# Cross attention's last block: score halves in turn, subtractions in a row, and block 13's last scaling and product behind the sums

## The chip, the cores and the metric

The kernel runs on one core of one Trainium2 chip. The metric is the device time of one execution in microseconds (us). A core has five engines that run side by side and wait for each other through semaphores: TensorE (PE in the profile, with its weight loads as PEld), VectorE (DVE), ScalarE (ACT), GpSimd (POOL) and SyncE (SP, which issues DMAs here).

## The reference, cut to what matters

One layer of a perceiver: cross attention of x to a long context, then self attention with relative positions, then a gated attention block. All in float32. The change is in the cross attention (and in the place of one step of the position table). What it computes:

```python
q = (layernorm(x) @ Wq + bq)        # x: 4 x 128 x 512, 16 heads of 32
k = (ctx @ Wk + bk)                 # ctx: 4 x 2048 x 512
v = (ctx @ Wv + bv)
scores = einsum('bqhd,bkhd->hbqk', q, k) / sqrt(32)
attn = softmax(scores.reshape(16 * 4, 128, 2048), axis=0)
x = x + einsum('hbqk,bkhd->bqhd', attn, v) @ Wo + bo
```

The softmax goes over heads and batch together (axis 0, 64 values for each pair of a query and a key), not over the keys. So each key's column is normalised by itself, and blocks of keys are independent until their products with v are added up.

## The kernel before, in words

The 2048 keys are cut into NK = 16 blocks of 128. In a block n the scores of all 16 heads and 4 batches are held as four tiles `sg[n, c]`, c = 0 to 3, of 128 keys by 2048 (4 heads x 4 batches x 128 queries). The order of the instructions on each engine is the order in which the program writes them (the section is under a manual schedule); the tile framework adds only the waits. The steps for one quarter (n, c), by function name and line:

- `keys` (L278) and `values` (L287): two projections of the context block on PE, four matmuls each, into one of two PSUM banks of a pool that they share (`bank`, L265); ACT copies the result out (L285, L291) and POOL adds the value's bias (L292). The v tiles have a pool of nine buffers.
- `scores` (L294): 16 small matmuls into two PSUM tiles of two banks each, called halves. `scores_out` (L314) is ACT's copy of one half to `sg`. `largest_of` (L317) is DVE's running maximum over one half, read from PSUM. In blocks 0 and 1 the program writes copy of half 1, maximum of half 0, copy of half 0, maximum of half 1. In later blocks it writes both copies first, and both maxima later, from `largest` (L326).
- `largest_tail` (L338) ends the maximum of a block on DVE (2 us). `shifted` (L345 through `over`) subtracts it from a quarter, `exponentials_of` (L354) is ACT's exponential of a quarter, `total` (L363) adds the quarter to the sum of its block on POOL, two folds of 128x1024 for a quarter (L360, L361), one for the first quarter (L358). `total_tail` (L371) ends the sum on POOL, `inverse` (L376) is DVE's reciprocal.
- `scaled` (L345 again) multiplies a quarter by the inverse on DVE; `attend` (L380) is the product with v, 16 matmuls of 32 columns, into a PSUM bank; `accumulate` (L396 on, L402 is its add) adds that bank to `acc` on DVE. Products without a bank of their own go to one bank with a single buffer, so each waits there for the accumulation of the one before.

The loop (L444) is a pipeline over blocks: in iteration n it makes the scores of block n, shifts and exponentiates block n-1, and scales and multiplies block n-2. A product is held back by one quarter (`done`): (n-2, c-1) is issued in quarter c. In the last iteration, n = 15, the values of block 15 begin (L450), since there are no keys left to make.

After the loop comes the tail (L493 on, m = 14, n = 15): the last product of block 13 (L494), block 15's maximum, shifts and exponentials with the remaining value projections between them, block 14's inverse and scalings. The sum of block 15 is divided: POOL adds quarters 0 and 1 and the first half of quarter 2 (`half_total`, L368), and PE adds the rest, and POOL's result, by products with the identity matrix into a PSUM bank (`sum_up`, L520). PE also puts x into the four output banks by identity products (L517). L538 folds the sum's bank to the normaliser z of block 15; then follow its inverse, the scalings of block 15, its products on top of block 14's in the same banks (`onto`), accumulations, and the output projection `project_out` (L542) in pieces between them. The next layer norm reads the output banks.

`position_table` (L110) is a generator whose three steps are placed in the first blocks: GpSimd's preparation (L438), a row product with its trip through DRAM (L469), and a product with a flip matrix, copied by ACT to `pos` (L141, L142), which the change moves. `pos` is first read in the self attention, at 708 us.

## Time and profile before

Three runs took 874.06, 872.05 and 871.6 us, median 872.05. The profiled execution took 871.75 us by itself; its span from the first to the last instruction is 869.8 us, at a mean granted clock of 0.986.

| engine | busy us | share of the span | instructions |
|---|---|---|---|
| PE | 831.1 | 96% | 7109 |
| DVE | 625.6 | 72% | 617 |
| ACT | 438.8 | 50% | 730 |
| POOL | 437.9 | 50% | 295 |

| part of the kernel, from the timelines | us from the span's start |
|---|---|
| first scores of block 0 | 44.6 |
| last scores (block 15, quarter 3) | 600.5 |
| normaliser of block 15 (L538) | 628.3 |
| first accumulation of block 15 | 633.6 |
| first statistics of the next layer norm | 653.2 |
| first projection of the self attention | 661.5 |

In the profile a row of the timeline is one instruction or a run of equal ones, with the idle time of its engine before it and the releaser in brackets. A busy share says little here, since it is the mean over stages; the order of the instructions is fixed on each engine, so the question at each point is which of several engines arrives last. The granted clock is PE's: at 0.50 the same matmul takes about twice as long.

### The profile page before, as it was taken

What the parts mean: (1) busy time and instruction counts of PE and PEld (TensorE: products, weight loads), DVE (VectorE), ACT (ScalarE), POOL (GpSimd) and SP (SyncE); (2) the same over time, 40 slices, a digit from 0 to 9 for tenths busy, and PEclk for the clock granted to TensorE, in tenths of its full rate; (3) what the DMA queues carried; (4) which work ended last, traced back from release to release, by engine and by line L of the source; (5) the groups of instructions that cost most, each with busy time, mean ns of one, the idle gap of its engine ahead of it and who ended that gap; (6) DMA issues with size and microseconds to landing.
All of it is one profiled execution on the core that took longest, in us unless ns stands there. A gap on an engine that the chain in (4) does not pass through costs nothing. (4 is left out here: it accounts for less than half of the span.)

```text
span 869.8 us, 16501 instructions
## 1 busy us (share of the span) xinstructions
PE 831.1 (96%) x7109; PEld 450.1 (52%) x7109; DVE 625.6 (72%) x617; ACT 438.8 (50%) x730; POOL 437.9 (50%) x295
## 2 busy tenths in 40 slices
PE   9999999999999999999999999999989996779998
PEld 5454544554544545545554544544445565566564
DVE  2049688888888888988878888888963537556563
ACT  3358446465465455455464464554403555844671
POOL 1246766666757567666566757567700022512152
PEclk9999999999999999999999999999999999789999
DMA  8140010110101001010110101001101203002101
GB/s 301 34 142 2 1 49 2 49 50 1 50 1 49 11 39 50 1 50 1 50 49 2 49 2 49 2 1 50 48 2 49 96 4 146 2 2 50 50 2 49
DMA packets 10906, 35.55 MB, mean 41 GB/s; under 512 B 977, under 2 KB 1138, under 8 KB 8786
## 3 DMA queue, kind: packets, MB, share of 16 engines
q1 hardware_dynamic: 8402, 29.43, 9.5%
q10 hardware_dynamic: 1632, 3.15, 1.0%
q0 software_dynamic: 800, 1.93, 0.9%
q8 instruction: 56, 0.92, 0.4%
q14 instruction: 16, 0.13, 0.0%
HBM read 33.45 MB, written 1.05 MB: 40 GB/s over the span
## 5 line engine op out<-in xcount | busy, mean ns | idle before, releaser
L345 DVE TENSOR_TENSOR sg<-sg,stat 128x2048 f32<-128x2048 f32 x128 | 288.2, 2281 | 1.2
L354 ACT ACTIVATE sg<-sg 128x2048 f32<-128x2048 f32 x64 | 122.4, 1912 | 244.9 <-DVE sg L345 244.9
L244 PE MATMUL ps_v<-w_xattn_Wv,ct 128*128 128x512 f32 x512 | 232.6, 598 | 3.6 <-ACT v L291 3.3
L237 PE MATMUL ps_k<-ct,w_xattn_Wk 128*128 128x512 f32 x480 | 221.9, 605 | 0.8 <-ACT pos L142 0.8
L360 POOL TENSOR_TENSOR sm<-sm,sg 128x1024 f32<-128x1024 f32 x46 | 108.6, 2360 | 145.5 <-ACT sg L354 143.3
L324 DVE TENSOR_TENSOR mx<-mx,ps_s 128x1024 f32<-128x1024 f32 x96 | 117.2, 1221 | 78.1 <-ACT sg L315 65.9
L244 PEld LDWEIGHTS ps_v<-w_xattn_Wv,ct 128*128 128x128 f32 x512 | 96.3, 191 | 130.6 <-issue 113.9
L237 PEld LDWEIGHTS ps_k<-ct,w_xattn_Wk 128*128 128x128 f32 x480 | 86.2, 189 | 94.1 <-issue 86.1
L315 ACT COPY sg<-ps_s 128x1024 f32<-128x1024 f32 x128 | 124.2, 1020 | 7.2 <-DVE mx L322 3.5
L361 POOL TENSOR_TENSOR sm<-sm,sg 128x1024 f32<-128x1024 f32 x46 | 108.8, 2366 | 3.6
L292 POOL TENSOR_TENSOR v<-v,row_xattn_bv 128x512 f32<-128x512 f32 x64 | 81.7, 1277 | 41.4 <-ACT v L291 38.0
L302 PE MATMUL ps_s<-qT,kT 32*128 32x128 f32 x2048 | 75.7, 283 | 0.1
L389 PEld LDWEIGHTS pso<-sg,v 128*32 128x32 f32 x1920 | 49.2, 110 | 47.5 <-DVE mx L324 22.0
L302 PEld LDWEIGHTS ps_s<-qT,kT 32*128 32x128 f32 x2048 | 63.3, 186 | 18.0 <-issue 17.0
L389 PE MATMUL pso<-sg,v 128*32 128x128 f32 x1920 | 65.3, 277 | 3.7 <-DVE acc L402 2.1
L358 POOL TENSOR_TENSOR sm<-sg 128x1024 f32<-128x1024 f32 x16 | 37.9, 2366 | 45.3 <-ACT sg L354 45.2
L656 POOL TENSOR_TENSOR lg<-lg,pos 128x512 f32<-128x512 f32 x6 | 7.4, 1263 | 85.9 <-ACT lg L655 85.9
L285 ACT ACTIVATE kT<-ps_k,bk 128x512 f32<-128x512 f32 x64 | 44.2, 694 | 11.9 <-PE ps_k L237 6.0
L291 ACT COPY v<-ps_v 128x512 f32<-128x512 f32 x64 | 36.4, 569 | 10.1 <-PE ps_v L244 10.1
L402 DVE TENSOR_TENSOR acc<-pso,acc 128x512 f32<-128x512 f32 x54 | 36.9, 682 | 3.9 <-PE pso L389 3.9
L322 DVE TENSOR_TENSOR mx<-sg,ps_s 128x1024 f32<-128x1024 f32 x16 | 19.5, 1220 | 27.3 <-ACT sg L315 27.3
L995 POOL TENSOR_TENSOR e<-e,rs 128x512 f32<-128x512 f32 x16 | 16.3, 1041 | 40.6 <-DVE rs L994 40.6
(213 smaller groups left out, 834.7 us busy)
## 6 DMA issues: line engine op xcount, KB each, us to landing
ct<-in_ctxT SPq DMA_DIRECT2D x15, 1024.0 KB, 4.9
ev_win<-in_tabv SPq DMA_DIRECT2D x1, 2048.0 KB, 9.3
w_xattn_Wk<-in_xattn_Wk ACTq DMA_DIRECT2D x4, 256.0 KB, 7.9
ct<-in_ctxT SPq DMA_DIRECT2D x4, 256.0 KB, 6.5
x<-in_x SPq DMA_DIRECT2D x4, 256.0 KB, 8.0
w_xattn_Wv<-in_xattn_Wv ACTq DMA_DIRECT2D x1, 1024.0 KB
w_xattn_Wq<-in_xattn_Wq SPq DMA_DIRECT2D x1, 1024.0 KB, 10.4
w_xattn_Wo<-in_xattn_Wo ACTq DMA_DIRECT2D x1, 1024.0 KB, 5.3
```

The lines of the kernel that those rows point to most:

```text
L237: nc.tensor.matmul(ps, lhsT=w[:, k, c * P : (c + 1) * P], rhs=src[:, k, :], start=(k == 0), stop=(k == C - 1))
L244: nc.tensor.matmul(ps, lhsT=src[:, k, b * T : (b + 1) * T], rhs=w[:, k, :], start=(k == 0), stop=(k == C - 1))
L285: nc.scalar.activation(kT[n, c], ps, AF.Identity, bias=bk[:, c : c + 1])
L292: nc.gpsimd.tensor_tensor(v[n, b], v[n, b], bv_row, ALU.add)
L302: nc.tensor.matmul(ps[i][:, cols], lhsT=kT[n, c][rows, cols], rhs=qT[rows, c, cols], start=True, stop=True)
L315: nc.scalar.copy(sg[n, c][:, k * HALF : (k + 1) * HALF], pss[n, c][k])
L324: nc.vector.tensor_tensor(mxs[n], mxs[n], pss[n, c][k], ALU.max)
L345: nc.vector.tensor_tensor(g, g, stat[:, row, :].unsqueeze(1).to_broadcast([P, NH * B, T]), op)
L354: nc.scalar.activation(sg[n, c], sg[n, c], AF.Exp, scale=SCALE)
L360: eng.tensor_tensor(t, t, g[:, 0:HALF], ALU.add)
L361: eng.tensor_tensor(t, t, g[:, HALF:], ALU.add)
L389: nc.tensor.matmul(ps[i * HD : (i + 1) * HD, b * T : (b + 1) * T], lhsT=v[n, b][:, h * HD : (h + 1) * HD], rhs=sg[n, c][:, f * T : (f + 1) ...
```

## The change

Nothing is computed differently in kind. The order in the last iteration and in the tail changes, and the sum of block 15 is divided otherwise between POOL and PE:

- Values 1 to 3 of block 15 go to the four temporary buffers that the layer norms use for `xn`, not to the pool of v tiles.
- The last scores, (15, 3), are copied and searched half by half in turn, as in blocks 0 and 1.
- In that quarter, exponential and sum of (14, 3) come behind the scores. A `break` leaves out the rest of it: scaling (13, 3) and accumulation (13, 2) move to the tail.
- The tail makes values 1 and 2 at once, then four subtractions in a row with their exponentials (values 3 behind the first), and only then scaling (13, 3), accumulation (13, 2), inverse of block 14 and scaling (14, 0).
- `half_total` is gone: POOL adds quarters 0 and 1, PE quarters 2 and 3 whole.
- The product (13, 3) comes behind the sums, its accumulation behind scaling (15, 0). Product (14, 0) has a bank of the shared pool, (14, 1) too; (14, 2) is in the single bank and comes behind product (15, 0).
- The third step of the position table comes at the end of block 0, not in block 1.

The diff:

```diff
         def values(n, b):
-            v[n, b] = vp.tile([P, D], F32, tag="v", name=f"v{n}_{b}")
+            if n == NK - 1 and b:
+                v[n, b] = tmp.tile([P, D], F32, tag="xn", name=f"v{n}_{b}")
+            else:
+                v[n, b] = vp.tile([P, D], F32, tag="v", name=f"v{n}_{b}")
...
             sg[n, c] = sc.tile([P, NH * B * T], F32, tag="sg", name=f"sg{n}_{c}")
-            if n < 2:
+            if n < 2 or (n, c) == (NK - 1, C - 1):
                 for k in (1, 0):
                     scores_out(n, c, k)
                     largest_of(n, c, 1 - k)
...
         def largest(n, c):
-            if n >= 2:
+            if n >= 2 and (n, c) != (NK - 1, C - 1):
                 largest_of(n, c, 0)
                 largest_of(n, c, 1)
...
-        def half_total(n, c):
-            nc.gpsimd.tensor_tensor(sms[n], sms[n], sg[n, c][:, 0:HALF], ALU.add)
...
                     shifted(n - 1, c)
-                    if n > 1:
+                    if n > 1 and (n, c) != (NK - 1, C - 1):
                         exponentials_of(n - 1, c)
                         total(n - 1, c)
...
                 if n == 0 and c == 0:
                     next(position)
+                if n == 0 and c == C - 1:
+                    next(position)
...
                     exponentials_of(0, c)
                     total(0, c)
-                    if c == 0:
-                        next(position)
+                if (n, c) == (NK - 1, C - 1):
+                    exponentials_of(n - 1, c)
+                    total(n - 1, c)
                 if n and c == C - 1:
                     total_tail(nc.gpsimd, n - 1)
                 if n >= 2:
                     if c == 0:
                         inverse(n - 2)
+                    if (n, c) == (NK - 1, C - 1):
+                        break
                     scaled(n - 2, c)
...
-        m, n = NK - 2, NK - 1
-        attend(*done)
+        l, m, n = NK - 3, NK - 2, NK - 1
         largest_tail(n)
         values(n, 1)
-        shifted(n, 0)
-        exponentials_of(n, 0)
-        total(n, 0)
+        values(n, 2)
+        for c in range(C):
+            shifted(n, c)
+            exponentials_of(n, c)
+            if c == 0:
+                values(n, 3)
+            if c < 2:
+                total(n, c)
+        scaled(l, C - 1)
         accumulate(*done)
-        values(n, 2)
-        shifted(n, 1)
-        exponentials_of(n, 1)
-        total(n, 1)
-        shifted(n, 2)
-        exponentials_of(n, 2)
-        values(n, 3)
-        half_total(n, 2)
-        shifted(n, 3)
-        exponentials_of(n, 3)
         inverse(m)
         scaled(m, 0)
-        scaled(m, 1)
...
-        sum_up(sg[n, 2][:, HALF:], True, False)
+        sum_up(sg[n, 2], True, False)
         sum_up(sg[n, 3], False, False)
         sum_up(sms[n], False, True)
-        attend(m, 0)
-        attend(m, 1, bank("m1"))
+        attend(l, C - 1)
+        attend(m, 0, bank("m0"))
+        scaled(m, 1)
         scaled(m, 2)
...
         inverse(n)
-        attend(m, 2, bank("m2"))
+        attend(m, 1, bank("m1"))
...
         scaled(n, 0)
+        accumulate(l, C - 1)
         attend(n, 0, pso[m, 0], True)
         accumulate(n, 0)
         scaled(n, 1)
+        attend(m, 2)
         project_out(0, range(B - 1))
         attend(n, 1, pso[m, 1], True)
```

## The prediction

> **What bounds the kernel now.** I read the busy shares first: PE 96%, DVE 72%, ACT and POOL 50%. The chain of waits is of no help ahead of 626 us; it starts there. So I read each engine's timeline over the change's stage, 590 to 656 us, and then the same span cut at the edges of the clock. DVE, from the last scores to the normaliser (columns: start, duration, line, operation, then in brackets the idle time before it and what ended it):

> ```profile
> 605.25 2.54 DVE L324 TENSOR_TENSOR mx<-mx,ps_s 128x1024 f32<-128x1024 f32 x2 [1.54 <-ACT sg L315]
> 607.83 1.95 DVE L339 TENSOR_REDUCE stat<-mx 128x128 f32<-128x1024 f32 x1
> 609.82 2.29 DVE L345 TENSOR_TENSOR sg<-sg,stat 128x2048 f32<-128x2048 f32 x1
> 612.02 0.68 DVE L402 TENSOR_TENSOR acc<-pso,acc 128x512 f32<-128x512 f32 x1
> 612.62 6.67 DVE L345 TENSOR_TENSOR sg<-sg,stat 128x2048 f32<-128x2048 f32 x3
> 619.40 0.96 DVE L376 RECIPROCAL stat<-z 128x128 f32<-128x128 f32 x1
> 620.40 6.68 DVE L345 TENSOR_TENSOR sg<-sg,stat 128x2048 f32<-128x2048 f32 x3
> 628.27 0.69 DVE L538 TENSOR_REDUCE z<-ps_sum 128x128 f32<-128x512 f32 x1 [1.19 <-PE ps_sum L523]
> ```

> DVE idles 1.54 us for ACT's copies of the last scores, then works without a break to 627.08. PE over the same time:

> ```profile
> 603.76 1.69 PE L389 MATMUL pso<-sg,v 128*32 128x128 f32 x32 [2.07 <-DVE acc L402]
> 605.38 11.60 PE L244 MATMUL ps_v<-w_xattn_Wv,ct 128*128 128x512 f32 x24
> ...
> 620.25 5.31 PE L523 MATMUL ps_sum<-sg,ident 128*128 128x512 f32 x12
> 626.25 1.98 PE L523 MATMUL ps_sum<-sm,ident 128*128 128x512 f32 x4 [0.69 <-POOL sm L369]
> ...
> 632.40 1.08 PE L389 MATMUL pso<-sg,v 128*32 128x128 f32 x32 [1.42 <-DVE sg L345]
> 634.30 4.54 PE L544 MATMUL ps_out<-w_xattn_Wo,acc 128*128 128x512 f32 x6 [0.81 <-DVE acc L402]
> ```

> The normaliser (628.27) waits for PE's last four sums, and these for POOL's half_total (L369). POOL's run depends on the exponentials, and they on the subtractions. The six projections at 634.30 take 0.76 us each; the same line's later ones follow each other every 0.43. The windows say why (columns: stretch, length, PE busy, PEld, DVE, ACT, POOL, granted clock, DMA share, GB/s):

> ```profile
> 600.69:604.10 3.41, 1.34 (x44) 1.15 (x48) 3.02 (x3) 3.09 (x3) 1.60 (x2) 1.00 0.00 0
> 604.10:607.51 3.41, 3.41 (x31) 1.99 (x24) 2.15 (x2) 1.12 (x2) 3.33 (x2) 0.50 0.02 5
> 631.41:634.82 3.41, 1.60 (x33) 1.11 (x34) 2.21 (x3) 0.00 (x0) 0.00 (x0) 1.00 0.00 0
> 634.82:638.23 3.41, 3.41 (x5) 1.35 (x4) 1.62 (x1) 0.00 (x0) 0.00 (x0) 0.50 0.00 0
> 720.15:723.57 3.42, 1.82 (x19) 1.61 (x16) 2.48 (x4) 0.00 (x0) 0.00 (x0) 1.00 1.05 385
> ```

> A stretch with PE busy 1.34 or 1.60 us of 3.41 (39%, 47%) is followed by one at half clock; one with 1.82 (53%) is not. Both half-clock stretches last 3.41 us and begin nine such lengths apart.

> **Part by part, ahead of the normaliser.** Times are on this profile's scale.

> *Last scores by halves.* They end at 600.52+1.17 = 601.69. For the alternation the row is the first block, which already has it:

> ```profile
> 51.04 2.54 DVE L324 TENSOR_TENSOR mx<-mx,ps_s 128x1024 f32<-128x1024 f32 x2 [2.96 <-PE ps_s L302]
> ```

> There the scores start at 49.83, DVE follows their end by 0.04 us, and the second ACT copy, at 52.29, waits for the first maximum. In that block's last scores the reduction follows their start by 63.09-59.30 = 3.79 us. So the reduction begins at 604.31 (was 607.83) and, 1.99 us later, the first subtraction at 606.30 (was 609.82): 3.5 us earlier. ACT's copies end at 603.99, and the exponential of block 14's last quarter, now behind them, at 605.8 (was 602.92).

> *Four subtractions in a row.* 2.29+3x2.20 = 8.9: 615.2. Then what was moved behind: scaling (13,3) 2.2, accumulation 0.7, inverse with its gap 1.0, three scalings 6.7: 625.8. DVE is ready for the normaliser then.

> *PE* no longer waits 2.07 us at 603.76: the product (13,3) is moved behind the sums, so the three value projections start at 601.7. Without the wait their stretch isn't under half busy, and 24x0.43 = 10.3: 612.0 (was 617.0). The identity products of x take 3.4: 615.4.

> *ACT.* Its in-order queue puts the copy of values 3 ahead of exponential 1. It ends at 612.7; three exponentials at 1.82 spacing end at 614.5, 616.35 and 618.2. The sums start at 616.4 and are 16 instead of 12, 16x0.43 = 6.9: 623.3.

> *POOL* loses half_total (2.36) but starts the fold of (14,3) at 605.85 instead of 603.06. Two folds 4.75, tail 2.58, three bias adds 3x1.24, one fold 2.35, two folds 4.75: 624.0. This is the last to arrive. PE's last four sums take 2.0: 626.05, and the normaliser starts at **626.07** (was 628.27): 2.2 us. The margins are thin: PE alone would allow 625.1, DVE 625.8.

> **Behind the normaliser.** Inverse and scaling follow as before, so product (15,0) starts at 630.20. PE waits 1.4 us for it as now. Its accumulation ends at 632.05; in its shadow PE does the moved product (14,2), 1.05, to 632.25, in place of the 0.81 wait. So the stretch has 1.4 us idle at most, at least 2.0 of 3.41 busy (59%), over the 1.82 that kept the clock. Six projections 6x0.43 = 2.57: 634.85; product (15,1) 1.05: 635.9; accumulation 0.7: 636.6; two scalings 4.45: 641.05; accumulation 0.65: 641.7. Before, this one ended at 645.61. **3.9 us**, of which 1.7 come behind the normaliser; from here on the order is the same.

> [...] The window rows show the drop after 1.60 us busy; I take the rows. [...] the grid may fall elsewhere in another run, and then before has no drop there to lose.

> *The position table's third step* moves from block 1 to the end of block 0. Its ACT copy (0.26 us, 71.23) delays the next by 0.15, and POOL's folds follow that exponential without a break to 93.15, where DVE waits for them: 0.15 us gained, bounds 0 and 0.26. The 0.81 us PE waits for that copy is worth nothing: at 131.71 PE waits 1.58 for ACT anyway. The moved product waits for nothing: POOL had seen posr landed by 55.34, and it is needed after 60.4.

> *At nothing:* values 1 to 3 in temporary buffers, last read by transposes before 27 us, next written after product (15,3) is done. Product (14,0) takes values 3's bank (copied 612.7), (14,1) the sum's (read 626.8, needed 627), (14,2) the single product bank (free 630.75, needed 631.2); (14,3) waits there for the accumulation ending 641.7, but PE comes to it at 644.3. Late banks would each cost the difference. SP's load of the next Wk, at 617.01, only waits for the last value projection and goes earlier; nothing is behind it.

> **Sum.** 3.9+0.15 = 4.05. The profiled execution took 871.75 (span 869.8 and 1.95 around it): 867.7. The median of the runs, 872.05, is 0.3 above it; I predict 868.0.

> **Rivals.**
> *A, as worked out:* 868.0, chance 0.62.
> *B, the clock part fails:* the grid spares the typical run before, or still catches the one after. For it: a margin of 0.2 us between 1.60 and 1.82, and a spread of 2.5 us over three runs. Against: the profiled run has the drop and is within 0.3 of the median. Gain 2.35: 869.7. Chance 0.24.
> *C, POOL keeps the old end:* its folds end at 626.2 again; only 1.7+0.15 remain: 870.2. For it: POOL is the last of three. Against: its durations hardly vary (2350 to 2390 ns). Chance 0.06.
> *D, more:* A with half-clock stretches of the later stages (740 to 747, 754 to 757, 778 to 785) falling shorter, 1.5 us: 866.5. Chance 0.05.
> *E, slower:* PE's clock is halved during the value projections. Then ACT's copy of values 3 holds up the exponentials: wholly at half clock projections end at 622.3, exponentials at 628.5, sums at 635.3, the normaliser 7.1 us later than before; less 1.85 this is 5.3 slower: 877.3. It decides from 4.9 us of delay at the projections (PE has 0.95 to spare, the whole gain is 3.9). Against: no wait is left ahead of them. Chance 0.03.

> **Range.** Within 0.3% is 2.6 us, about what a measurement can tell from no change: 869.4 to 874.7. A lies below in nine of ten (0.57), B in four of ten (0.10), D wholly: faster 0.73. Same: the rest of A and B and C, 0.24. Slower: E, 0.03. The low end takes D, the high end B and C: 866.3 to 870.6.

> **What would show it.** The first subtraction 3.5 us earlier, four in a row; no PE idle time ahead of the value projections; the last sums waiting for POOL, the normaliser 2.2 us earlier; the first six projections every 0.43 us; the moved product between (15,0) and them. Wrong if PE waits again for ACT or a bank, or the stretch after the sums is under half busy.

## The result, and the profile after

| kernel | median of 20 runs, us | lowest to highest | profiled execution (span) |
|---|---|---|---|
| before | 872.0 | 869.43 to 874.06 | 871.75 (869.8) |
| after | 868.5 | 867.86 to 872.27 | 870.22 (868.3) |

The ratio of the times is 0.9974, with a 95% interval of 0.9963 to 0.9985: 2.3 us less, between 1.3 and 3.2. This is the distance of the means of the 20 runs (871.5 and 869.2). The medians lie 3.5 us apart. That these two numbers differ, and that the two profiled executions are only 1.5 us apart, is the main question below.

DVE's timeline after, in the same stretch as the one shown of before (line numbers have moved: L328 is the maximum, L349 subtraction and scaling, L539 the normaliser):

```profile
600.99 2.55 DVE L328 TENSOR_TENSOR mx<-mx,ps_s 128x1024 f32<-128x1024 f32 x2 [0.81 <-PE ps_s L306]
603.57 1.97 DVE L343 TENSOR_REDUCE stat<-mx 128x128 f32<-128x1024 f32 x1
605.58 11.08 DVE L349 TENSOR_TENSOR sg<-sg,stat 128x2048 f32<-128x2048 f32 x5
616.57 0.68 DVE L403 TENSOR_TENSOR acc<-pso,acc 128x512 f32<-128x512 f32 x1
617.17 0.95 DVE L377 RECIPROCAL stat<-z 128x128 f32<-128x128 f32 x1
618.16 6.68 DVE L349 TENSOR_TENSOR sg<-sg,stat 128x2048 f32<-128x2048 f32 x3
625.72 0.69 DVE L539 TENSOR_REDUCE z<-ps_sum 128x128 f32<-128x512 f32 x1 [0.88 <-PE ps_sum L523]
```

The maximum now waits for the scores, not for ACT. The run of five is the four subtractions and scaling (13,3). The last scores start at 599.78 here and at 600.52 before, so times are compared from there: the first subtraction comes 5.80 us behind them (9.30 before), the normaliser 25.94 (27.75). PE, after:

```profile
600.88 10.57 PE L244 MATMUL ps_v<-w_xattn_Wv,ct 128*128 128x512 f32 x24
611.29 3.60 PE L517 MATMUL ps_out<-x,ident 128*128 128x512 f32 x8
615.74 7.13 PE L523 MATMUL ps_sum<-sg,ident 128*128 128x512 f32 x16 [0.85 <-ACT sg L358]
623.70 1.98 PE L523 MATMUL ps_sum<-sm,ident 128*128 128x512 f32 x4 [0.83 <-POOL sm L365]
...
629.88 1.08 PE L390 MATMUL ps_m<-sg,v 128*32 128x128 f32 x32 [1.45 <-DVE sg L349]
630.78 1.06 PE L390 MATMUL pso<-sg,v 128*32 128x128 f32 x32
631.78 2.84 PE L545 MATMUL ps_out<-w_xattn_Wo,acc 128*128 128x512 f32 x6
```

No wait is left ahead of the value projections. The last four sums wait for POOL, as forecast. The moved product (630.78) fills PE's time up to the projections, and six of these take 2.84 us instead of 4.54.

But for the position table's step the rest of the kernel wasn't touched. The whole of each profiled execution, in stretches:

| from, to (us) | before | after |
|---|---|---|
| start to last scores of block 0 | 59.30 | 58.66 |
| last scores of block 0 to last scores of block 15 | 541.22 | 541.12 |
| last scores of block 15 to normaliser | 27.75 | 25.94 |
| normaliser to first statistics of the next layer norm | 24.95 | 23.28 |
| these statistics to the first projection of self attention | 8.28 | 8.37 |
| first projection of self attention to the end | 208.3 | 210.9 |

The tail gained 1.81 and 1.67 us; self attention, with the same instructions, lost 2.6. The 0.64 us at the start is not the change's: nothing was moved there, and over the eleven profiles of this case this stretch takes 58.42 to 59.53 us. Two neighbouring stretches of the clock in self attention, after (columns as in the prediction's window rows):

```profile
715.39:718.80 3.41, 1.81 (x33) 1.49 (x30) 2.49 (x4) 0.00 (x0) 0.06 (x1) 1.00 0.89 300
718.80:722.22 3.42, 3.42 (x40) 3.09 (x40) 0.00 (x0) 0.00 (x0) 0.00 (x0) 0.50 1.07 452
```

The second is a half-clock stretch that the profile of before doesn't have. PE was busy for 1.81 us ahead of it; the row of before with 1.82 us was followed by full clock. So at 1.81 and 1.82 us (53%) PE's busy time does not tell whether the clock falls.

### The profile page after: what moved, and what is told of

It reads as the page before. It is cut to its first block, busy times and chain, and to the rows that moved or that the text cites. A ratio compares the mean times of both kernels' runs of the same rounds, so it can differ in the third digit from the quotient of the medians.

```text
span 868.3 us, 16503 instructions
## 1 busy us (share of the span) xinstructions
PE 831.1 (96%) x7113; PEld 451.0 (52%) x7113; DVE 625.5 (72%) x617; ACT 438.8 (51%) x730; POOL 435.8 (50%) x294
## 3 DMA queue, kind: packets, MB, share of 16 engines
HBM read 33.45 MB, written 1.05 MB: 40 GB/s over the span
## 4 chain that ended last, share of the span: by engine, by line
DVE 34%; PE 34%; ACT 20%; issue 10%; POOL 2%; DVEq 0%; ACTq 0%; POOLq 0%
DVE sg L349 14%; DVE mx L328 11%; ACT sg L319 10%; PE ps_v L244 4%; ACT sg L358 3%; PE s_k L237 3%; DVE stat L343 3%; ACT v L295 3%; PE ps_k L237 3%; DVE mx L326 2%; PE s_v L671 2%; PE s_y L1085 2%; PE s_q L237 2%; PE ps_q L237 2%; PE s_q L244 2%
## 5 line engine op out<-in xcount | busy, mean ns | idle before, releaser
L349 DVE TENSOR_TENSOR sg<-sg,stat 128x2048 f32<-128x2048 f32 x128 | 288.1, 2282 | 1.2
L244 PE MATMUL ps_v<-w_xattn_Wv,ct 128*128 128x512 f32 x512 | 231.5, 596 | 3.7 <-ACT v L295 3.7
L328 DVE TENSOR_TENSOR mx<-mx,ps_s 128x1024 f32<-128x1024 f32 x96 | 117.2, 1221 | 77.2 <-ACT sg L319 64.2
L244 PEld LDWEIGHTS ps_v<-w_xattn_Wv,ct 128*128 128x128 f32 x512 | 95.8, 190 | 129.9 <-issue 112.8
```

The costliest lines, as they stand in the source:

```text
L244: nc.tensor.matmul(ps, lhsT=src[:, k, b * T : (b + 1) * T], rhs=w[:, k, :], start=(k == 0), stop=(k == C - 1))
L328: nc.vector.tensor_tensor(mxs[n], mxs[n], pss[n, c][k], ALU.max)
L349: nc.vector.tensor_tensor(g, g, stat[:, row, :].unsqueeze(1).to_broadcast([P, NH * B, T]), op)
```

## The experiments

**Does the clock differ between runs of one kernel?** The kernel before, unchanged.

> The kernel before, unchanged, for a second trace and for each run's granted clock. Theory (grid): the windows of the clock lie anew in each run, so times fall in groups some 2 us apart (869.5, 872, 874 so far), the groups with the lower mean clock are the slower ones, and a run of the 869.5 group has a mean clock near 0.99 instead of 0.986. Rival (fixed): the clock is the same in each run, and the spread has another cause, so clock and time do not go together.

The ratio to the kernel before is 1.0003, from 0.9991 to 1.0015. Clock and time go together in its 22 runs:

| mean granted clock | runs | us |
|---|---|---|
| 0.990 | 4 | 869.02 to 869.52 |
| 0.986 or 0.987 | 12 | 870.87 to 872.57 |
| 0.983 or 0.984 | 6 | 872.10 to 874.55 |

Its profiled execution was one of 869.17. PE behind the sums in it:

```profile
631.57 1.08 PE L389 MATMUL pso<-sg,v 128*32 128x128 f32 x32 [1.42 <-DVE sg L345]
633.46 2.84 PE L544 MATMUL ps_out<-w_xattn_Wo,acc 128*128 128x512 f32 x6 [0.81 <-DVE acc L402]
```

Both waits stand there, 1.42 and 0.81 us as in the first profile, and yet the projections run at full clock: 2.84 us. From the normaliser to the next layer norm's first statistics it takes 23.25 us, as much as the changed kernel (23.28). There is no half-clock stretch at 604 either, and the normaliser comes 27.73 us behind the last scores, so the one there in the first profile cost nothing. The grid theory holds: reduced by whole stretches of 3.41 us, the edges of the clock lie 0.8 us from the span's start here and 3.3 us in the first profile. The rival falls. Four profiles have this tail without fillers (the two of before and two experiments below), and only the first has the drop in it.

**Is it PE's waiting that costs the clock?** Fill the two waits.

```diff
+        def keep_busy(k):
+            for _ in range(k):
+                nc.tensor.matmul(out_ps[0][:, 0:P], lhsT=warm, rhs=warm, start=False, stop=False)
...
+        keep_busy(5)
         attend(n, 0, pso[m, 0], True)
+        keep_busy(3)
         accumulate(n, 0)
```

> The kernel before with only PE kept busy in the two waits behind the normaliser: 5 and 3 matmuls that add zeros to an output bank (1.1 and 0.65 us) in the waits of 1.42 and 0.81 us. Theory (grid): no half-clock stretch at the first six projections, which follow each other every 0.43 us; from the normaliser to the accumulation of product (15,2) some 1.7 us less than in the profile of before (17.3 from start to start instead of 16.65 is ruled out: 14.9 to 15.0 in place of 16.65), and the group of runs at 872 shrinks, with a median near 870.0. Rival (the 1.7 us come from the new order of the products, not from the clock): 16.65 us as before, median 872.

```profile
630.44 1.38 PE L544 MATMUL ps_out<-warm 128*128 128x128 f32 x10
631.93 1.08 PE L389 MATMUL pso<-sg,v 128*32 128x128 f32 x32
632.94 0.94 PE L544 MATMUL ps_out<-warm 128*128 128x128 f32 x6
633.82 2.84 PE L548 MATMUL ps_out<-w_xattn_Wo,acc 128*128 128x512 f32 x6
```

`warm` holds zeros, so nothing is added. The waits are filled, nothing comes later, and from the normaliser to the accumulation of (15,2) it is 14.96 us, to the statistics 23.25. The ratio is 0.9986 (0.9974 to 0.9998), some 1.2 us less, with a median of 870.67, not 870.0. So the tail's part of the clock can be had with no reordering at all, and on the mean of runs it is worth somewhere between 0.2 and 2.3 us. An estimate narrows it. These are two positions of a stretch over the two waits in the second profile of before, the outermost with as little PE work as the 1.58 us ahead of the drop in the first (1.60 in the prediction's row, whose edges are 0.02 us off):

```profile
629.65:633.06 3.41, 1.58 (x52) 1.04 (x43) 2.21 (x2) 0.00 (x0) 0.00 (x0) 1.00 0.02 5
630.55:633.96 3.41, 1.58 (x33) 1.11 (x34) 2.21 (x3) 0.00 (x0) 0.00 (x0) 1.00 0.00 0
```

They lie 0.90 us apart, a quarter of 3.41. With 1.83 us as the limit, which kept the clock at 128.30 us in the profile of after, it is 1.40 us, four tenths; 1.88 us kept the clock at this place in the experiment with the position table's step alone. If all positions are equally likely, before has the drop in a quarter to four tenths of its executions, and it costs 0.4 to 0.7 us on average, not 1.7.

**Where did self attention lose its 2.6 us?** The changed kernel with PE kept busy there, and, for comparison, the kernel before with both sets of fillers. The edit of the later stage:

```diff
+        fill = bank_z("fill")[:, 0:P]
+        idle(fill, 6)
         ps = logits(0)
...
             if c + 1 < C:
+                if c < 2:
+                    idle(fill, 6)
                 ps = logits(c + 1)
...
                 if c:
+                    idle(fill, {(1, 3): 22, (2, 3): 3, (3, 0): 5}.get((c, i), 0))
                     transposed(c - 1, i)
...
+        idle_ps = bank_z("idle")[:, 0:P]
+        idle(idle_ps, 21)
         out_ps = [bank_q(f"out{b}") for b in range(B)]
...
-        idle_ps = bank_z("idle")[:, 0:P]
```

> The changed kernel with PE kept busy in the waits of the self attention's logits, exponentials and output (6 matmuls of zeros ahead of the first three sets of logits, 22, 3 and 5 ahead of three transposes, 21 ahead of the output's transposes), into a bank that nothing reads. Theory (grid): the half-clock stretches between 715 and 785 us go, at most one is left; self attention becomes shorter by 2 to 5 us, the mean clock over 0.995, and the runs' spread falls from 4.4 us to about 1; median 864 to 866. Rival (the later stages lost 2.7 us in the profiled execution through the change itself, its earlier weight loads for instance): they stay as long as in the profile of after, median 868 to 870.

> The kernel before with both sets of filling matmuls, those of the tail and those of the later stages. Theory (grid): a narrow spread like that of the changed kernel with the later filling, and slower than it by the order part of the change alone, 1.9 us (1.6 to 2.3). Rival (fixed): slower than it by 3.5 to 4.1 us.

| kernel | median us (6 runs each) | lowest to highest | self attention to the end, profile |
|---|---|---|---|
| before, both fillings | 867.81 | 867.30 to 868.18 | 206.28 |
| after, later filling | 865.59 | 865.24 to 866.59 | 206.71 |

The spread falls from about 5 us to 0.9 and 1.4, self attention is equal but for 0.4 us in both, and one half-clock stretch is left there in the changed kernel's profile, none in the other's. With the clock held so far, the change gains **2.2 us** (2.1 between the means), inside the forecast of 1.6 to 2.3 for its order part; the rival (3.5 to 4.1) falls. The later loss was the clock's, not the change's. The changed kernel's own runs say the same: 12 of the 20 had a mean clock of 0.990 (the profiled one 0.986) and took 867.86 to 868.51 us.

**Which edits carry the order part?** Four kernels with one thing changed each. First, the halves undone: both copies first, then both maxima.

```diff
-            if n < 2 or (n, c) == (NK - 1, C - 1):
+            if n < 2:
                 for k in (1, 0):
                     scores_out(n, c, k)
                     largest_of(n, c, 1 - k)
+            elif (n, c) == (NK - 1, C - 1):
+                for k in (1, 0):
+                    scores_out(n, c, k)
+                largest_of(n, c, 0)
+                largest_of(n, c, 1)
```

> The changed kernel with one part undone: the last scores are copied whole by ACT first, and both maxima follow. Theory (POOL's folds arrive last): the first subtraction comes 1.1 to 1.3 us later against the start of the last scores, but the exponential of (14,3) and POOL's run start up to 0.2 us earlier, so the normaliser is only 0.2 to 0.6 us later (26.1 to 26.5 us behind the start of the last scores instead of 25.94), then with DVE's scalings as the last arrival. Rival (the subtractions set the end): the normaliser is later by the same 1.1 to 1.3 us.

```profile
603.40 2.55 DVE L333 TENSOR_TENSOR mx<-mx,ps_s 128x1024 f32<-128x1024 f32 x2 [2.88 <-ACT sg L324]
605.98 1.96 DVE L348 TENSOR_REDUCE stat<-mx 128x128 f32<-128x1024 f32 x1
607.97 11.08 DVE L354 TENSOR_TENSOR sg<-sg,stat 128x2048 f32<-128x2048 f32 x5
...
620.55 6.68 DVE L354 TENSOR_TENSOR sg<-sg,stat 128x2048 f32<-128x2048 f32 x3
627.15 0.68 DVE L544 TENSOR_REDUCE z<-ps_sum 128x128 f32<-128x512 f32 x1
```

The last scores start at 600.12, so the first subtraction is 7.85 us behind them, 2.05 later than with the halves and not 1.1 to 1.3: the first maximum waits for both copies, since the half that it reads is copied last. The normaliser is 1.09 later (27.03). It now follows the scalings without a wait: DVE is the last to arrive, and of the 2.05 us DVE's former wait of 0.88 for PE took up most (0.96 with the 0.08 by which the two rows now overlap). Neither forecast holds: the theory's 0.2 to 0.6 us was too small, and the rival's 1.1 is met only as a number, since the subtraction moved by 2.05. That DVE would be the last was right: the halves are worth 1.1 us. The product behind the normaliser waits 2.33 us in this kernel, and the clock is half from 631.0 to 634.4.

Second, only the removal of half_total, in the kernel before.

```diff
-        half_total(n, 2)
...
-        sum_up(sg[n, 2][:, HALF:], True, False)
+        sum_up(sg[n, 2], True, False)
```

> The kernel before with one part of the change alone: no half_total on POOL, PE adds quarter 2 whole. Theory (the parts hold each other up): POOL is done 2.4 us earlier, but PE has four sum instructions more, and its value projections and identity products still end some 5 us later than in the changed kernel, so the normaliser stays within 0.4 us of before (27.75 us behind the start of the last scores). Rival (POOL's half_total alone held it up): 1.5 to 2.2 us earlier.

```profile
603.14 1.08 PE L389 MATMUL pso<-sg,v 128*32 128x128 f32 x32 [2.07 <-DVE acc L402]
604.15 10.57 PE L244 MATMUL ps_v<-w_xattn_Wv,ct 128*128 128x512 f32 x24
614.55 3.60 PE L516 MATMUL ps_out<-x,ident 128*128 128x512 f32 x8
618.53 7.13 PE L522 MATMUL ps_sum<-sg,ident 128*128 128x512 f32 x16 [0.38 <-ACT sg L354]
625.50 1.88 PE L522 MATMUL ps_sum<-sm,ident 128*128 128x512 f32 x4
```

The last four sums wait for nothing now, but PE itself is late. The normaliser comes 27.52 us behind the last scores, 0.23 earlier (0.21 against the second profile of before, which has full clock in the projections as this one has), and the rival's 1.5 to 2.2 falls. Third, the opposite: half_total put back into the changed kernel.

```diff
             if c < 2:
                 total(n, c)
+            if c == 2:
+                nc.gpsimd.tensor_tensor(sms[n], sms[n], sg[n, c][:, 0:HALF], ALU.add)
...
-        sum_up(sg[n, 2], True, False)
+        sum_up(sg[n, 2][:, HALF:], True, False)
```

> The changed kernel with half_total back on POOL (first half of quarter 2), and PE adding the second half alone. Theory (POOL's folds arrive last): POOL ends one fold, 2.4 us, later, PE's last four sums wait for it, and the normaliser comes 2.3 to 2.5 us later, 28.2 to 28.4 us behind the start of the last scores, which is later than in the kernel before (27.75): without this edit the rest of the new order loses 0.5 us ahead of the normaliser. Rival (the earlier subtractions carry the gain): it stays at 26 to 26.5.

```profile
615.68 5.50 PE L525 MATMUL ps_sum<-sg,ident 128*128 128x512 f32 x12 [0.85 <-ACT sg L358]
626.04 3.68 PE L525 MATMUL ps_sum<-sm,ident 128*128 128x512 f32 x4 [4.87 <-POOL sm L511]
```

POOL ends 26.26 us behind the last scores, 2.39 later, as the theory said. But PE waits 4.87 us for it, and its four sums then take 3.68 instead of 1.98, at half clock: the normaliser comes at 30.04, another 1.7 later than expected. So an edit worth 0.23 us by itself is worth 4.1 once the others are made (2.4 of it without the clock).

Fourth, the position table's step alone, in the kernel before.

```diff
                 if n == 0 and c == 0:
                     next(position)
+                if n == 0 and c == C - 1:
+                    next(position)
...
-                    if c == 0:
-                        next(position)
```

> The kernel before with the position table's third step at the end of block 0. From the start of block 0's last scores to the inverse of block 0 (33.89 us before): 0.15 to 0.25 us less; PE's wait of 0.81 us at the third set of keys of block 1 is gone and its wait in front of block 2's or block 3's products grows by about as much. A rival that counts PE's wait would have the last scores come 0.8 us earlier, too; by this theory they do by 0.1 to 0.25.

From the last scores of block 0 to its inverse it takes 33.68 us (33.89 before, 33.69 after): 0.21. PE's wait of 0.81 is gone and comes back: in the first profile PE waited 0.22 us for scaling (0,0) in block 2; here it waits there 0.88. The row before, then here:

```profile
96.53 1.08 PE L389 MATMUL pso<-sg,v 128*32 128x128 f32 x32 [0.22 <-DVE sg L345]
96.54 1.08 PE L389 MATMUL pso<-sg,v 128*32 128x128 f32 x32 [0.88 <-DVE sg L345]
```

The last scores of block 15 follow those of block 0 by 541.15 (541.16 to 541.33 in the five profiles of kernels with the step at its old place, 540.91 to 541.12 in the five of the changed kernel and its variants). So some 0.1 to 0.2 us, as forecast, and not 0.8. (The 541.15 of this single profile stands within 0.01 us of the other group; the 0.21 at the inverse is the firmer number.)

**A version that beats both.** POOL was last by less than a microsecond over PE and DVE, so one fold of it was given to PE, into PE's wait of 0.85 us, in the changed kernel with the later filling.

```diff
-            if c < 2:
+            if c == 0:
                 total(n, c)
+            if c == 1:
+                nc.gpsimd.tensor_tensor(sms[n], sms[n], sg[n, c][:, 0:HALF], ALU.add)
...
-        sum_up(sg[n, 2], True, False)
+        sum_up(sg[n, 1][:, HALF:], True, False)
+        sum_up(sg[n, 2], False, False)
```

> The changed kernel with later filling as in the earlier run, and besides POOL relieved of one more fold: the second half of quarter 1 is summed by PE, ahead of quarter 2, where PE waited 0.85 us. Theory (POOL last, PE and DVE close behind): POOL ends 2.4 us earlier and no longer decides, PE's sums end 0.3 to 0.6 us earlier, the normaliser 25.4 to 25.7 us behind the start of the last scores instead of 25.94; median 0.2 to 0.6 us below 865.6. Rival (POOL's time is worth itself): 1 us or more below.

```profile
615.45 8.75 PE L525 MATMUL ps_sum<-sg,ident 128*128 128x512 f32 x20
624.03 1.88 PE L525 MATMUL ps_sum<-sm,ident 128*128 128x512 f32 x4
```

No wait is left between or ahead of the sums. The normaliser comes at 25.45, 0.49 earlier; the median of 5 runs is 865.26, 0.33 below the same kernel without this edit (timed apart from it, so without an interval; the kernel before was 0.1 lower there, too), and 0.9926 (0.9907 to 0.9945) of the kernel before. Most of that distance is the change and the fillers; POOL's fold of 2.4 us bought half a microsecond in the profile, since PE was next.

## Why the prediction was right, and where it wasn't

- *What bounds the stage.* Right. POOL was the last, as the row at 623.70 shows, and held PE up by 0.83 us. In three of the four single edits there (halves undone, half_total removed, one fold more for PE) another engine then decided; where half_total was put back, POOL alone did.
- *Last scores by halves.* Right: the first subtraction came 3.50 us earlier, forecast 3.5. Half undone, 2.05 of it came back.
- *The normaliser 2.2 us earlier.* It was 1.81. The mis-sized term is POOL's sum. I took 4.75 us for two folds and 2.35 for one from places where a bias add of another tile follows. Here folds of the same tile follow each other, at 2.45 us from start to start: 4.89, 2.45 and 4.82 in place of 4.75, 2.35 and 4.75, and the start 0.1 later, make the 0.4. POOL, after:

```profile
605.20 2.36 POOL L364 TENSOR_TENSOR sm<-sm,sg 128x1024 f32<-128x1024 f32 x1 [3.46 <-issue]
607.64 2.37 POOL L365 TENSOR_TENSOR sm<-sm,sg 128x1024 f32<-128x1024 f32 x1
610.09 2.08 POOL L338 TENSOR_TENSOR sm<-sm 128x512 f32<-128x512 f32 x2
...
616.38 2.37 POOL L362 TENSOR_TENSOR sm<-sg 128x1024 f32<-128x1024 f32 x1
618.83 2.37 POOL L364 TENSOR_TENSOR sm<-sm,sg 128x1024 f32<-128x1024 f32 x1
621.28 2.37 POOL L365 TENSOR_TENSOR sm<-sm,sg 128x1024 f32<-128x1024 f32 x1
```

- *Behind the normaliser 1.7.* Right for the pair of profiles: 1.67. In the way that the prediction used it, wrong. "I take the rows" was sound: in that profile the stretch with most of the waits of 1.42 and 0.81 us had 1.58 us of PE work and was followed by half clock, and so was the one with 1.2 us in the first single edit, where PE waited 2.33 us. The step that failed is the last one, "The profiled execution took 871.75 ...: 867.7. The median of the runs ... I predict 868.0". It took a drop that one execution had as one that every run has. The prediction named the reason itself, that the grid may fall elsewhere in another run, gave it 0.24, and set against it that the profiled run was near the median. This was no evidence: an execution can be as slow without the tail's drop, through drops in self attention (the fourth single edit's took 874.51 us with the tail at full clock). Without the drop the tail behind the normaliser takes as long in both kernels, 23.25 and 23.28 us: nothing of the 1.7 belongs to the order.
- *The margin of the clock.* The prediction counted a stretch with 2.0 us of PE work as safe, since 1.82 had kept the clock. The changed tail did keep it, with 1.97 us at the least in its profile. But the margin was no margin: in self attention 1.81 us, and in one experiment 2.12, were followed by half clock.
- *The sum.* The order part is 1.8 + 0.1 to 0.2, measured as 2.2 us with the clock held. The clock's part comes on top in those runs of before that have the drop. The measured 2.3 us (1.3 to 3.2) lies at the gain of rival B (2.35); A's 4.05 is outside. That the median of 868.5 is next to A's 868.0 is in good part luck: run times come in groups, and 12 of the 20 runs after are in the fastest (867.86 to 868.51), but only six of the 20 before (869.43 to 869.64). So the median of before lies a group higher, while within the fastest group the kernels are about 1.3 us apart. Which stretches the runs without a profile had is not known, so how much of this shift of groups is the change's own doing stays open. (In the range, the shares for faster add up to 0.72, not 0.73.)
- *Position table.* Right: 0.2 at its place, 0.1 to 0.2 at the end, and PE's wait was worth nothing. It came back sooner than said, at 96.5 us and not at 131.71.
- *What was costed at nothing* (temporary buffers, banks, the earlier weight load) shows no wait in the profile of after.

## What to carry to other kernels

Where several engines end close together, an edit's worth is set by the others: price it by the gap to the next arrival, not by its own length, and an edit that is worth little alone can be worth much together with others (0.23 and 4.1 us here). A half-clock stretch in one profile is a property of that execution until a second profile shows it too (the tail's stood in the first profile of before and not in its second); take it out of the sum, or hold the clock by filling PE's waits in both kernels before comparing them (the runs' spread fell from about 5 us to 0.9 and 1.4 here). A wait of an engine that is late by another's doing (PE's 0.81 us) came back here at another wait soon after.

## What the runs showed of the hardware

At a granted clock of 0.50 PE's last four sums took 3.68 us (half_total put back), at full clock 1.98 (after).

```profile
715.89:719.30 3.41, 2.12 (x65) 1.88 (x64) 1.25 (x3) 0.58 (x1) 1.53 (x2) 1.00 0.52 159
719.30:722.71 3.41, 3.23 (x16) 3.26 (x16) 1.23 (x3) 0.00 (x0) 0.00 (x0) 0.50 1.08 427
...
601.33:604.74 3.41, 1.60 (x34) 1.17 (x35) 1.87 (x3) 3.26 (x4) 2.31 (x1) 1.00 0.00 0
604.75:608.16 3.41, 3.41 (x10) 1.50 (x9) 3.27 (x3) 0.27 (x1) 3.33 (x3) 1.00 0.02 5
```

So PE's busy time, as the profile shows it, does not settle it alone there; what else does stays open. For the pair of waits of 1.42 and 0.81 us it mattered where they fell: in the first profile most of both lay in one stretch, with 1.58 us of PE work, and half clock followed; in the second of the same kernel each lay in a stretch of its own, with 1.99 and 2.61 us, and the clock stayed full. Filling PE's waits with matmuls of zeros took the half-clock stretches in self attention from between five and seven (the seven profiles without them there) to one or none, and brought 3.9 us in the median of the kernel before (871.7 to 867.8, its tail filled too) and 2.9 in that of the changed one, more than the change itself.
